# Eight gathers on SyncE instead of four, with table parts loaded in between

## The chip, the core and the metric

The kernel runs on one core of a Trainium2 chip. The metric is the device time of one execution in microseconds (us), as a median over runs. The core has five engines that run their own instruction streams in order: TensorE (PE; its weight loads are PEld), VectorE (DVE), ScalarE (ACT), GpSimd (POOL) and SyncE (SP, which here only issues DMA transfers). They meet at semaphores. Sixteen DMA engines move data between the memory of the chip (HBM) and the on-chip buffers.

## What is computed

A sequence of item numbers `seq` (1024 users, 50 steps) picks rows of 128 numbers from a table with 100001 rows, of which row 0 counts as zero:

```python
e = emb[seq]                                   # 1024 x 50 x 128
prefix = jnp.cumsum(e, axis=1)
uF = prefix / jnp.minimum(t_idx, lengths)      # running mean
y = (uF - mean) * rsqrt(var + eps) * gamma + beta   # mean, var over the users
# 50 steps of: v = v + (x - v) / 2; spike = v >= 1; v = v - spike
uF_out = spikes.mean(axis=0)                   # 1024 x 128
scores = uF_out @ emb.T                        # 1024 x 100001, float32
```

The output has 409.6 MB, and all of the table (51 MB) is read once for the last product, besides the single rows that the 51200 item numbers pick.

## The kernel before

The work has two stages.

In the first stage a loop over t = 0 to 49 (L300) makes one step at a time. `gather(t)` (L201) fills the tile e of 128 x 1024 with the rows of the 1024 items of step t. It does so with eight indirect DMAs, one for each block of 128 users, which GpSimd issues (L204). Two such tiles exist (pool gather, two buffers), so GpSimd works on step t + 1 while step t is used. PE transposes each block into the running sums `pre` in PSUM (L313, eight transposes, the first four into one half and the last four into the other). VectorE scales the two halves and takes their statistics (L322, L323), aggregates them (L333), and a chain of small VectorE and ScalarE instructions makes the normalised input and the new state v (L337 to L359). In the last step (t = 49) the spikes of the step before are taken first (L307, L308), and then the two halves. PE also adds a correction for row 0 (`correct`, L268), which needs `zT`, made at the start.

At the start of the stage VectorE compares idx with zero (L220), PE transposes the result (L223), ScalarE copies it (L225), VectorE makes a tile rb of reciprocal lengths (L240), and PE transposes that (L243). The tiles isz and rb of this start come from the same pool as e; the gathers of step 1 go into the buffer that rb used, and wait for L243.

SyncE issues in this order: the item numbers idx (L171), the lengths, row 0, gamma and beta (L173 to L178), then six DMAs of 3 MB each that bring the first 36 parts of the table (a part is 1024 rows, 0.5 MB) into the tiles rows (`fetch`, L97), and after them single rows. For t = 44 to 47 the block of the first 128 users is not gathered by GpSimd: SyncE reads four item numbers of a user into registers (L189), and issues one DMA of one row (512 bytes) for each (L197), into four tiles aside. So 128 register loads of four values and 512 row loads. Each SyncE DMA uses one of eight semaphores in turn, and waits until the DMA that used it before has landed.

In the second stage the table parts are transposed and split in two (`prepare`, L133; parts 0 and 1 already in steps 42 and 44 of the first stage), multiplied with the spike counts (`product`, L146), scaled into tiles o (L471, L473), and stored by SyncE (`store`, L157). The first store comes from L408, at the end of the first stage. Later parts of the table are fetched on ScalarE's queue.

The order of the instructions on each engine is the order in which the program writes them.

Of the kernel before, what the change touches and what calls it, by code (L numbers as in the profile page):

```python
# [12 lines left out]
F32 = mybir.dt.float32  # L13
BF16 = mybir.dt.bfloat16
F32R = mybir.dt.float32r
I32 = mybir.dt.int32
U32 = mybir.dt.uint32
AF = mybir.ActivationFunctionType
ALU = mybir.AluOpType

P = 128
# [5 lines left out]
GROUP = 6  # L27
AHEAD = 6

WIDTHS = [2, 2, 2, 3, 3, 3, 3] + 12 * [6] + [4, 4]  # L30
NARROW, MIDDLE = 3, 7


@with_exitstack
def rec_kernel(
# [9 lines left out]
    nc = tc.nc  # L45
    B, T = seq.shape
    N, D = table.shape
# [25 lines left out]
    rows = {}  # L73
# [6 lines left out]
    def size(q):  # L80
        return min(HALF, N - q * HALF)

    def group(g):
        at = g if g < AHEAD else AHEAD - 2 + g % 2
        r = rowp.tile([P, GROUP, HALF], F32, tag=f"rows{at}", name=f"rows_{g}")
        for k in range(GROUP):
            rows[g * GROUP + k] = r[:, k, :]
        return r

    def fetch(r, q, n):  # L90

        engine = nc.sync if q < AHEAD * GROUP else nc.scalar
        k = q % GROUP
        n = min(n, parts - q)
        whole = n - (size(q + n - 1) < HALF)
        if whole:
            engine.dma_start(  # L97
                out=r[:, k : k + whole, :],
                in_=table[q * HALF : (q + whole) * HALF, :].rearrange("(q p k) d -> p q (k d)", p=P, k=KQ),
            )  # L100
        if whole < n:
            full, rest = divmod(size(parts - 1), P)
            c1 = (parts - 1) * HALF
            r = r[:, k + whole, :].rearrange("p (k d) -> p k d", d=D)
            if full:
                engine.dma_start(
                    out=r[:, :full, :],
                    in_=table[c1 : c1 + full * P, :].rearrange("(k p) d -> p k d", p=P),
                )
            if rest:  # L110
                engine.dma_start(out=r[:rest, full, :], in_=table[c1 + full * P : N, :])
# [49 lines left out]
    with ExitStack() as ph:  # L161
        once = ph.enter_context(tc.tile_pool(name="once", bufs=1))
        lp = ph.enter_context(tc.tile_pool(name="lif", bufs=2))
        sp = ph.enter_context(tc.tile_pool(name="stats", bufs=3))
        up = ph.enter_context(tc.tile_pool(name="uF", bufs=2))
        gp = ph.enter_context(tc.tile_pool(name="gather", bufs=2))
        accp = ph.enter_context(tc.tile_pool(name="acc", bufs=1, space=bass.MemoryType.PSUM))
        vp = ph.enter_context(tc.tile_pool(name="v", bufs=1, space=bass.MemoryType.PSUM))

        idx = once.tile([P, NB, T], I32, tag="idx", name="idx")  # L170
# [5 lines left out]
        gb = once.tile([P, 2], F32, tag="gb", name="gb")  # L176
        nc.sync.dma_start(out=gb[:, 0:1], in_=gamma.rearrange("(d o) -> d o", o=1))
        nc.sync.dma_start(out=gb[:, 1:2], in_=beta.rearrange("(d o) -> d o", o=1))  # L178
        for g in range(AHEAD):
            fetch(group(g), g * GROUP, GROUP)  # L180

        aside = {}
        for t0, many in ((T - 6, 4),):
            for t in range(t0, t0 + many):
                aside[t] = once.tile([P, P], F32, tag=f"aside{t}", name=f"aside_{t}")
            for p in range(P):
                _, items = nc.values_load_multi_w_load_instructions(  # L189
                    idx[p : p + 1, 0, t0 : t0 + many],  # L190
                    engines=[mybir.EngineType.SP],
                    min_val=0,
                    max_val=N - 1,
                    skip_runtime_bounds_check_because="items are rows of the table; the transfer checks its own bounds",
                )
                for j, item in enumerate(items):
                    nc.sync.dma_start(out=aside[t0 + j][p : p + 1, :], in_=table[bass.ds(item, 1), :])  # L197

        es = {}

        def gather(t):  # L201
            es[t] = gp.tile([P, B], F32, tag="e", name=f"e_{t}")
            for n in range(t in aside, NB):
# [3 lines left out]
                    in_=table,  # L207
                    in_offset=bass.IndirectOffsetOnAxis(ap=idx[:, n, t : t + 1].bitcast(U32), axis=0),
                )
# [52 lines left out]
        def only(t):  # L262

            l = sp.tile([P, D], F32R, tag="l", name=f"l_{t}")
            nc.scalar.activation(l, r0n, AF.Copy, scale=sel[:, t : t + 1])
            return l
# [33 lines left out]
        for t in range(T):  # L300
# [35 lines left out]
            r = sp.tile([P, 1], F32, tag="r", name=f"r_{t}")  # L336
            nc.scalar.activation(r, mv[:, 1:2], AF.Sqrt, bias=eps)  # L337
            nc.scalar.activation(uF, uF, AF.Identity, bias=mv[:, 0:1], scale=-1.0)

# [11 lines left out]
            a = sp.tile([P, 1], F32, tag="a", name=f"a_{t}")  # L351
# [3 lines left out]
            def x(vt, cs):  # L355
                nc.scalar.activation(vt, uF[:, cs], AF.Identity, bias=hgb[:, 1:2], scale=a)  # L356

# [41 lines left out]
        for q, (pool, tag, po) in enumerate(((gp, "e", sums), (up, "uF", [po1[:, cs] for cs in halves]))):  # L399
            o = pool.tile([P, HALF], F32, tag=tag, name=f"o_0_{q}")  # L400
# [26 lines left out]
    for c, W in enumerate(WIDTHS):  # L427
# [30 lines left out]
        for n in range(NB):  # L458
            if c == 0 and n == 0:
                continue  # L460
            pool, tag, most = turns[blocks % len(turns)]
            blocks += 1
            o = pool.tile([P, most * HALF], F32, tag=tag, name=f"o_{c}_{n}")
# [21 lines left out]
            if n in (1, 4) and c >= MIDDLE and to_fetch < parts:  # L485
                g = to_fetch // GROUP
# [26 lines left out]
```

## Time and profile before

| what | before |
|---|---|
| median of 3 runs | 1779.58 us (1778.25 to 1783.5) |
| span of the profiled execution | 1569.9 us |
| POOL busy | 374.6 us in 402 instructions |
| DVE busy | 940.7 us in 1161 instructions |
| PE busy | 1153.1 us in 4548 instructions |
| DMA | 488.25 MB, mean 311 GB/s |

The span goes from the first to the last instruction of the profiled execution. The run times are longer than it by what lies around it; the profiled execution has no time of its own beside its span. In the rows of a timeline the first number is the start in us from the span's start, the second the duration, then engine, source line, operation, output and inputs, sizes, and in brackets the idle time of the engine before it and what ended it. An engine name with a q (SPq) is that engine's own instruction queue.

### The profile page before, as it was taken

To read this page: it belongs to the slowest core of one execution; us is meant where nothing else is said; L and a number is where in the kernel's file an instruction comes from. 1 tells how busy PE (TensorE), PEld (TensorE's weight loads), DVE (VectorE), ACT (ScalarE), POOL (GpSimd) and SP (SyncE) were. 2 spreads that over 40 slices of the span, in tenths; PEclk is the share of its full clock that TensorE was granted. 3 is DMA by queue.
4 is the path that set the end of the run, shared out by engine and by line. 5 is a ranking of instruction groups with operands and counts; after the bars stand their busy time and mean duration, and the time that the engine had idled before them with its cause. 6 is when DMAs were issued, how large, how long until landed. Compare 5 with 4: busy or idle time off the path is not lost.

```text
span 1569.9 us, 14231 instructions
## 1 busy us (share of the span) xinstructions
PE 1153.1 (73%) x4548; PEld 822.3 (52%) x4548; DVE 940.7 (60%) x1161; ACT 630.6 (40%) x700; POOL 374.6 (24%) x402
## 2 busy tenths in 40 slices
PE   4555555555556988899878788887788888788784
PEld 2222222222233766677666666666666666666563
DVE  4777777777778665576545555555555545555453
ACT  2322222222233554465444444444444444444342
POOL 6777777777775000000000000000000000000000
PEclk7555555555555999999999988999999998989998
DMA  9622222222222999999999999999999999999998
GB/s 342 245 55 53 55 54 54 54 53 54 52 53 64 399 411 420 420 393 428 425 432 427 429 428 424 418 422 424 428 413 420 415 424 429 421 423 409 394 423 354
DMA packets 54600, 488.25 MB, mean 311 GB/s; under 512 B 12443, under 2 KB 13756, under 8 KB 33276
## 3 DMA queue, kind: packets, MB, share of 16 engines
q1 hardware_dynamic: 33008, 429.03, 65.1%
q0 software_dynamic: 12672, 25.98, 6.2%
q10 hardware_dynamic: 8844, 32.33, 5.2%
q8 instruction: 36, 0.59, 0.1%
q14 instruction: 40, 0.33, 0.1%
HBM read 77.69 MB, written 409.60 MB: 310 GB/s over the span
## 4 chain that ended last, share of the span: by engine, by line
DMA 52%; POOL 17%; PE 11%; issue 9%; ACT 5%; DVE 4%; DVEq 0%; ACTq 0%; SPq 0%; POOLq 0%
DMA scores<-o 49%; POOL e L204 17%; PE po L149 9%; ACT o L473 5%; DMA e<-in_L_rec_emb_table,idx 3%; DVE o L471 2%; PE pt L119 1%; DVE bs L323 1%; DVE uF L322 0%; DVE s L343 0%; PE pre L313 0%; PE sums L281 0%; DMA idx<-in_r_seq 0%; ACT hi L141 0%; ACT pairs L141 0%
## 5 line engine op out<-in xcount | busy, mean ns | idle before, releaser
L471 DVE TENSOR_SCALAR o<-po 128x1024 f32<-128x1024 f32 x391 | 463.5, 1220 | 351.8 <-DMA scores<-o 323.4
L473 ACT ACTIVATE o<-po 128x1024 f32<-128x1024 f32 (+1 forms) x391 | 387.9, 1018 | 547.8 <-DMA scores<-o 344.9
L204 POOL DMA_INDIRECT e<-in_L_rec_emb_table,idx x396 | 373.9, 944 | 123.4 <-issue 114.6
L149 PE MATMUL po<-pairs,countB 128*128 128x512 f32 x1168 | 314.7, 415 | 67.6 <-ACT o L473 50.7
L149 PEld LDWEIGHTS po<-pairs,countB 128*128 128x128 f32 x1168 | 225.8, 198 | 132.5 <-ACT o L473 65.8
L149 PE MATMUL po<-pairs,countC 128*128 128x512 f32 x876 | 239.1, 419 | 43.6 <-ACT o L473 43.6
L313 PE MATMUL pre<-ident,e 128*128 128x128 f32 x396 | 153.1, 450 | 143.8 <-DMA e<-in_L_rec_emb_table,idx 142.2
L149 PEld LDWEIGHTS po<-pairs,countC 128*128 128x128 f32 x876 | 170.1, 200 | 89.7 <-ACT o L473 54.7
L313 PEld LDWEIGHTS pre<-ident,e 128*128 128x128 f32 x396 | 78.5, 201 | 236.1 <-DMA e<-in_L_rec_emb_table,idx 214.7
L142 DVE TENSOR_TENSOR pairs<-pt,pairs 128x1024 fp32r<-128x1024 f32 (+1 forms) x73 | 88.3, 1217 | 96.6 <-ACT pairs L141 96.5
L337 ACT ACTIVATE r<-mv,eps 128x1 f32<-128x1 f32 x50 | 14.7, 295 | 300.6 <-DVE mv L333 300.6
L322 DVE SCALAR_TENSOR_TENSOR uF<-rlen,pre 128x512 f32<-128x512 f32 x100 | 68.3, 683 | 103.8 <-PE pre L313 103.8
L119 PE MATMUL pt<-ident,rows 128*128 128x128 f32 x782 | 113.5, 293 | 8.0 <-ACT o L473 3.9
L119 PEld LDWEIGHTS pt<-ident,rows 128*128 128x128 f32 x782 | 102.6, 154 | 28.8 <-issue 10.0
L149 PE MATMUL po<-hi,countB 128*128 128x512 f32 x200 | 82.8, 414 | 18.8 <-ACT o L473 13.8
L281 PE MATMUL sums<-s,ident_h 128*128 128x512 bf16 x98 | 49.6, 608 | 60.6 <-DVE s L343 60.6
L270 PE MATMUL pre<-zT,l 128*128 128x512 f32 x100 | 78.0, 782 | 21.6 <-DVE uF L322 21.5
L149 PE MATMUL po<-lo,countB 128*128 128x512 f32 x200 | 80.4, 402 | 0.0
L141 ACT CAST pairs<-pt 128x1024 fp32r<-128x1024 f32 (+1 forms) x73 | 73.6, 1008 | 16.2 <-PE pt L119 15.9
L149 PE MATMUL po<-pairs,countA 128*128 128x512 f32 (+1 forms) x292 | 73.2, 393 | 9.1 <-ACT o L473 9.1
L149 PE MATMUL po<-hi,countC 128*128 128x512 f32 x150 | 62.7, 418 | 16.4 <-ACT o L473 16.4
L356 ACT ACTIVATE v<-uF,hgb,a 128x1024 f32<-128x1024 f32 x49 | 59.2, 1208 | 37.4 <-DVE a L352 37.4
(78 smaller groups left out, 821.1 us busy)
## 6 DMA issues: line engine op xcount, KB each, us to landing
scores<-o SPq DMA_DIRECT2D x96, 3072.0 KB
scores<-o SPq DMA_DIRECT2D x32, 1536.0 KB
rows<-in_L_rec_emb_table ACTq DMA_DIRECT2D x20, 1536.0 KB
scores<-o SPq DMA_DIRECT2D x22, 1024.0 KB
rows<-in_L_rec_emb_table SPq DMA_DIRECT2D x6, 3072.0 KB
scores<-o SPq DMA_DIRECT2D x8, 2048.0 KB
scores<-o SPq DMA_DIRECT2D x8, 1872.5 KB
aside<-in_L_rec_emb_table SPq DMA_DIRECT2D x512, 0.5 KB
```

Source lines behind the costliest of these rows:

```text
L119: nc.tensor.transpose(pt[:, k0 : k0 + kw], r[:kw, k0 : k0 + D], ident[:kw, :kw])
L141: nc.scalar.copy(vh, vp)
L142: nc.vector.tensor_tensor(vl, vp, vh.bitcast(F32), ALU.subtract)
L149: nc.tensor.matmul(po[:, :kw], lhsT=counts[n], rhs=part[:, k0 : k0 + kw], start=j == 0, stop=j == 1,)
L204: nc.gpsimd.indirect_dma_start(out=es[t][:, n * P : (n + 1) * P], out_offset=None, in_=table, in_offset=bass.IndirectOffsetOnAxis(ap=idx[: ...
L270: nc.tensor.matmul(pre[h], lhsT=l, rhs=zT[:, h * BANK : (h + 1) * BANK], start=t == 0, stop=False, skip_group_check=True,)
L281: nc.tensor.matmul(sums[h], lhsT=ident_h, rhs=s[:, h * BANK : (h + 1) * BANK], start=t == 0, stop=t == T - 2, skip_group_check=True,)
L313: nc.tensor.matmul(pre[h][:, k : k + P], lhsT=aside[t] if h == k == 0 and t in aside else e[:, h * BANK + k : h * BANK + k + P], rhs=ident ...
L322: nc.vector.scalar_tensor_tensor(uF[:, cs], rlen[:, cs], 1.0 / (t + 1), pre[h], ALU.max, ALU.mult)
L356: nc.scalar.activation(vt, uF[:, cs], AF.Identity, bias=hgb[:, 1:2], scale=a)
L471: nc.vector.tensor_scalar_mul(o[:, h0 : h0 + hw], po[:, :hw], 1.0 / T)
L473: nc.scalar.mul(o[:, h0 : h0 + hw], po[:, :hw], 1.0 / T)
```

## The change

Eight steps (t = 7, 13, 19, 25, 31, 37, 43 and 49) instead of four leave the first block of 128 users to SyncE. Their item numbers come by an additional small DMA into a tile few (8 partitions x 128 numbers), and VectorE multiplies them by 512, the bytes of a row. SyncE loads sixteen of these byte addresses into registers at a time, and uses them directly as starts in a byte view of the table. The aside tiles come from a pool of three buffers. The first 36 table parts are issued one by one (36 DMAs of 0.5 MB instead of six of 3 MB), spread evenly between the row loads. `gather` and the rest of the kernel are unchanged; the condition in `gather` and in the loop of t picks the steps from the dictionary `aside`. `group` and `fetch` are those of before.

```diff
--- before.py
+++ after.py
@@ -15,6 +15,7 @@
 F32R = mybir.dt.float32r
 I32 = mybir.dt.int32
 U32 = mybir.dt.uint32
+U8 = mybir.dt.uint8
 AF = mybir.ActivationFunctionType
 ALU = mybir.AluOpType
 
@@ -29,6 +30,8 @@
 
 WIDTHS = [2, 2, 2, 3, 3, 3, 3] + 12 * [6] + [4, 4]
 NARROW, MIDDLE = 3, 7
+
+ASIDE, EVERY, MANY = 8, 6, 16
 
 
 @with_exitstack
@@ -164,6 +167,7 @@
         sp = ph.enter_context(tc.tile_pool(name="stats", bufs=3))
         up = ph.enter_context(tc.tile_pool(name="uF", bufs=2))
         gp = ph.enter_context(tc.tile_pool(name="gather", bufs=2))
+        asidep = ph.enter_context(tc.tile_pool(name="aside", bufs=3))
         accp = ph.enter_context(tc.tile_pool(name="acc", bufs=1, space=bass.MemoryType.PSUM))
         vp = ph.enter_context(tc.tile_pool(name="v", bufs=1, space=bass.MemoryType.PSUM))
 
@@ -176,25 +180,38 @@
         gb = once.tile([P, 2], F32, tag="gb", name="gb")
         nc.sync.dma_start(out=gb[:, 0:1], in_=gamma.rearrange("(d o) -> d o", o=1))
         nc.sync.dma_start(out=gb[:, 1:2], in_=beta.rearrange("(d o) -> d o", o=1))
-        for g in range(AHEAD):
-            fetch(group(g), g * GROUP, GROUP)
-
-
-
+        held = [group(g) for g in range(AHEAD)]
+        to_hold = 0
+
+
+        steps = list(range(T - 1 - EVERY * (ASIDE - 1), T, EVERY))
+        few = once.tile([ASIDE, P], I32, tag="few", name="few")
+        with nc.allow_non_contiguous_dma(reason="a few columns of item numbers, once"):
+            nc.sync.dma_start(out=few, in_=seq[:P, steps[0] : T : EVERY].rearrange("p t -> t p"))
+        nc.vector.tensor_single_scalar(few, few, 4 * D, ALU.mult)
+        flat = table.rearrange("n d -> (n d)").bitcast(U8)
         aside = {}
-        for t0, many in ((T - 6, 4),):
-            for t in range(t0, t0 + many):
-                aside[t] = once.tile([P, P], F32, tag=f"aside{t}", name=f"aside_{t}")
-            for p in range(P):
-                _, items = nc.values_load_multi_w_load_instructions(
-                    idx[p : p + 1, 0, t0 : t0 + many],
+        for g, t in enumerate(steps):
+            aside[t] = asidep.tile([P, D], F32, tag="aside", name=f"aside_{t}")
+            for p0 in range(0, P, MANY):
+                while to_hold * ASIDE * P <= (g * P + p0) * AHEAD * GROUP and to_hold < AHEAD * GROUP:
+                    fetch(held[to_hold // GROUP], to_hold, 1)
+                    to_hold += 1
+                _, at = nc.values_load_multi_w_load_instructions(
+                    few[g : g + 1, p0 : p0 + MANY],
                     engines=[mybir.EngineType.SP],
                     min_val=0,
-                    max_val=N - 1,
-                    skip_runtime_bounds_check_because="items are rows of the table; the transfer checks its own bounds",
+                    max_val=(N - 1) * 4 * D,
+                    skip_runtime_bounds_check_because="these are starts of rows of the table; the transfer checks its own bounds",
                 )
-                for j, item in enumerate(items):
-                    nc.sync.dma_start(out=aside[t0 + j][p : p + 1, :], in_=table[bass.ds(item, 1), :])
+                for k, byte in enumerate(at):
+                    nc.sync.dma_start(
+                        out=aside[t][p0 + k : p0 + k + 1, :].bitcast(U8),
+                        in_=flat[bass.ds(byte, 4 * D)].rearrange("(o b) -> o b", o=1),
+                    )
+        while to_hold < AHEAD * GROUP:
+            fetch(held[to_hold // GROUP], to_hold, 1)
+            to_hold += 1
 
         es = {}
```

## The prediction

> **What bounds the kernel now.** I read the page first, then the rows of tile e, then the timelines of the two ends of the first stage, then SyncE's rows.
>
> ```profile
> span 1569.9 us, 14231 instructions
> ...
> POOL 6777777777775000000000000000000000000000
> ...
> DMA  9622222222222999999999999999999999999998
> ...
> DMA scores<-o 49%; POOL e L204 17%; PE po L149 9%; ACT o L473 5%; DMA e<-in_L_rec_emb_table,idx 3%; DVE o L471 2%; PE pt L119 1%; DVE bs L323 1%; DVE uF L322 0%; DVE s L343 0%; PE pre L313 0%; PE sums L281 0%; DMA idx<-in_r_seq 0%; ACT hi L141 0%; ACT pairs L141 0%
> ```
>
> There are two stages. Up to slice 13 (about 500 us) POOL works at a steady share and the DMA engines at 20%; after it POOL is idle and the DMA engines stand at 90% or more with the stores of the scores (49% of the chain). The change touches only the first stage. I take the 1063 us from the first store (506.8) to the end as unchanged, since the stores bound them.
>
> ```profile
> L204 POOL DMA_INDIRECT e<-in_L_rec_emb_table,idx x396: 940/944/1162, 4.3 to 497.6; - x198
> ...
>   issue: 114.6, 376
> ...
> DMA to landing us min/median/max: 2.4/2.5/6.8
> ```
>
> 396 gathers from 4.3 to 497.6 us: 0.944 us busy and 0.30 us of "issue" each, no other wait of weight. (497.64 − 4.30) / 395 = 1.249 us per gather: POOL never stops and sets the pace, 8 gathers or 9.98 us a step.
>
> ```profile
> 490.18 0.48 PE L313 MATMUL pre<-ident,e 128*128 128x128 f32 x1 [0.76 <-DMA e<-in_L_rec_emb_table,idx]
> ...
> 497.64 0.94 POOL L204 DMA_INDIRECT e<-in_L_rec_emb_table,idx  x1 [0.30 <-issue]
> ...
> 498.25 1.22 DVE L308 TENSOR_TENSOR negv<-s,v 128x1024 f32<-128x1024 bf16 x1
> ...
> 500.26 0.47 PE L313 MATMUL pre<-ident,e 128*128 128x128 f32 x1 [0.89 <-DMA e<-in_L_rec_emb_table,idx]
> ...
> 500.77 0.69 DVE L322 SCALAR_TENSOR_TENSOR uF<-rlen,pre 128x512 f32<-128x512 f32 x1
> ...
> 506.78 65.38 SPq L158 DMA_DIRECT2D scores<-o  x30
> ```
>
> This is the end of the stage. The last transpose of step 48 starts at 490.18 (call it X). From there VectorE works without a gap through step 48's tail to L308, which ends at 499.47; only then can it take both halves of step 49 (second half at 500.77). The last transpose of step 49 ends at 500.73, so gathers and VectorE arrive together. Up to X the stage is POOL's; from X on it is VectorE's as well.
>
> ```profile
> 1.04 0.91 DVE L218 MEMSET isz<- 128x1024 f32 x1 [1.04 <-PEq L501]
> ...
> 3.83 33.42 SPq L97 DMA_DIRECT2D rows<-in_L_rec_emb_table  x6
> 4.13 0.65 DVE L220 TENSOR_SCALAR isz<-idx 128x400 f32<-128x400 int32 x2 [2.18 <-DMA idx<-in_r_seq]
> 4.30 1.16 POOL L204 DMA_INDIRECT e<-in_L_rec_emb_table,idx  x1 [2.99 <-DMA idx<-in_r_seq]
> ...
> 10.30 1.97 PE L243 MATMUL rps<-ident,rb 128*128 128x128 f32 x8 [3.43 <-DVE rb L240]
> ...
> 13.26 0.94 POOL L204 DMA_INDIRECT e<-in_L_rec_emb_table,idx  x1 [0.30 <-issue]
> ...
> 14.51 0.94 POOL L204 DMA_INDIRECT e<-in_L_rec_emb_table,idx  x1 [0.30 <-issue]
> ```
>
> VectorE waits for idx (issued at 0.76), compares at 4.13, and a chain over PE, ACT and DVE ends in the transposes L243 at 12.27. POOL's ninth gather (14.51) writes the buffer that these transposes read, so it may not start before they end. Today that leaves 2.2 us of slack.
>
> **What the Trainium skill says.** "DMA: Bandwidth & Descriptors", Latency and other measured facts, gives a register load (tensor_load) a floor of about 600 ns, amortised by loading four at a time. "Runtime: NRT & Kernel Launch", Instruction fetch mechanics, says about 200 ns per register even in bulk, for loads from HBM. They pull apart: a floor makes sixteen values nearly as cheap as four, a price per register does not. The trace has four values from SBUF at 564 ns: below the floor, and 141 ns per register, so it decides nothing. The DMA page, Why a DMA increments its semaphore by 16 and not by 1, says that the engine count is the largest up to 16 that divides the slowest dimensions: the new few load (8 x 128) would run on 8 engines; no load of before has this shape.
>
> **The change, part by part.**
> *Gathers removed.* Before, steps 44 to 47 skip one gather each; after, steps 7, 13, ..., 43, 49. Up to X it is 4 before and 7 after: 3 x 1.249 = 3.7 us earlier. The eighth (step 49) lies after X: its 1.25 us on POOL are hidden behind VectorE, which is late next. Value 0, at most 1.25.
>
> *The start.* The few load (1024 pieces of 4 bytes) goes out at 3.83, in the place of the first table load, and VectorE's first instruction is now its multiplication. Behind it in VectorE's queue stand L218 and L220, for which PE, ACT and, by the buffer, POOL wait. idx (1024 pieces) took 3.37 us from issue to its user, len_i (1024 pieces of 4 bytes, by semaphore events) 3.07; few so lands at 6.9 to 7.2, and up to 8.6 if half the engines double the 1.5 us of its pieces. I take 7.4. Then multiplication about 0.2 (an estimate from the row of L233, 0.23), memset 0.91, and the compare starts at 8.6 instead of 4.13: 4.5 late. L243 ends at 16.8, the ninth gather starts at 16.9 instead of 14.51. Cost 2.4 us, bounds 1.9 to 3.6; below nothing is excluded, because POOL has no idle time later to win it back.
>
> ```profile
> L189 SPq TENSOR_LOAD <-idx x128: 457/564/737, 37.3 to 354.3; - x128
> L197 SPq FUSED_REGOPS  x512: 37/37/51, 37.9 to 356.2; - x171
> L197 SPq MOVE aside<-in_L_rec_emb_table x512: 29/29/29, 38.0 to 356.2; - x171
> L197 SPq DMA_DIRECT2D aside<-in_L_rec_emb_table x512: 224/225/7507, 38.0 to 356.3; - x171
> 100.15 256.36 SPq L197 DMA_DIRECT2D aside<-in_L_rec_emb_table  x441
> ```
>
> *SyncE.* 441 row loads took 256.36 us: 0.581 each. By start times in the trace a load is FUSED_REGOPS to MOVE 73 ns, MOVE to DMA 60, DMA to the next 276; a TENSOR_LOAD takes 564 + 54, and 46 more in what follows. 4 x 409 + 664 = 2.30 us for four; a pause of some 0.35 us about every 23 us makes the rest. After: the scaling on chip removes the FUSED_REGOPS, so sixteen loads cost 16 x 336 = 5.38, plus 0.10, plus T, the TENSOR_LOAD of sixteen. 64 of these: 350 + 64 T. The table parts: 36 DMAs of 128 runs, like the gb loads at 0.43 + 0.05: 17. Each SyncE DMA waits for the eighth before it; a row lands 1.1 to 1.5 us after issue and eight take 2.7, a 0.5 MB part needs about 3.2 (1.5 at the 342 GB/s of slice 1, plus start and receipt) against 3.2 and a TENSOR_LOAD: no wait. Pauses: 7. Sum S = 374 + 64 T, starting at 7.7.
>
> *When it must be ready.* The last group (step 49) has to land so that four transposes (1.4 us) end when VectorE is free, 499.5 − 1.3: at 496.8. With 1.4 to land, S may be 487.7, so T may be 1.78 us. The earlier groups need their rows every 58.6 us (47 gathers), looser than that because the first has until about 80 us. If T is 0.56, S is 410; if T grows by register (16 x 0.141 = 2.26), S is 519 and the stage ends 31 us late; at the page's 0.2 per register T is 3.2 and it would be 91. I take T = 1.2, between the trace's fixed and proportional readings: S = 451, last row at 460, hidden behind POOL with 37 us to spare. If that cover goes, each 0.1 us of T costs 6.4.
>
> *Table parts in between, three aside buffers, multiplication.* The parts 0 and 1 are wanted at step 42 and 44 (over 400 us), the rest in the second stage; the last is issued at about 450: nothing. A buffer is reused 18 steps later, after PE read it 100 us before: nothing. Gathers meet a 1.5 us part now and then, and have a whole step of buffer: nothing. The multiplication itself is counted above.
>
> **Sum.** −3.7 + 2.4 = −1.3 us: span 1568.6 against 1569.9. The median of the runs, 1779.58, lies 209.7 above the profiled span; I take that as constant: 1778.3.
>
> **The rivals.**
> A, forecast: SyncE keeps up, the start costs 2.4: 1778.3; own range 1774 to 1782. 0.52.
> B, slower: the TENSOR_LOAD of sixteen is priced by the register. Place: SyncE, between groups; it decides from T = 1.78, and at 2.26 gives −1.3 + 31 = +30: 1809 (at T = 2.0, 1794). For it: the price per register, and 564 / 4. Against: 564 is below a floor of 600 for one. 0.35.
> C, the start does not cost (few lands early or the ninth gather is not held), and perhaps the tail gives its 1.25: −3.7 to −5.0: 1775.2. For it: only that 2.2 us of slack exist; against: the queue order on VectorE. 0.10.
> D, the change does not do what it says: the byte-typed copies go out as 512 pieces instead of one 512-byte run. At the 9 ns of a 4-byte piece that is 4.6 us for each of 1024 loads, 4.2 ms more. Against: a contiguous row was one piece before. 0.03.
>
> **How the numbers follow.** What a measurement can tell from no change is about 0.3%, 5.3 us. A and C lie inside it (their gains are 1.3 to 5.0), 0.62, of which I give 0.05 to faster, since C stands at the edge and the runs shown spread over 5 us; B beyond T = 1.86 and D make slower 0.36; a B between 1.78 and 1.86 stays in same. Same 0.59. The range runs from 1774 (C) to 1808, which takes in most of B; A's own is given above.
>
> **What would show it.** Right: SyncE's rows at about 0.42 us a load and ending near 460; the TENSOR_LOAD at 0.6 to 1.7; compare L220's start near 8.6 and the ninth gather near 16.9; POOL ending 4 gathers less 2.4, so 2.6 us, before its old 498.6; the first store near 505.5. Wrong: PE or POOL waiting for a DMA of tile aside, a SyncE row that runs past 496, a TENSOR_LOAD over 1.8, more packets under 512 B than the few load adds, or a second stage of another length than 1063 us.

## The result, and the profile after

The changed kernel took 1847.1 us (median, 1843.5 to 1849.5) against 1779.3 for the kernel before: a ratio of 1.0365, interval 1.0341 to 1.0388, 68 us slower. The forecast was 1778.3 and no change. Without a difference in the program, the kernel before takes 1780 us in all runs of some sessions and 1571 in all runs of others: this comparison is of the first kind, and the profile of before that the prediction was read from is of the second.

The page of the changed kernel, in the session of the comparison (span, then busy tenths of POOL in 40 slices of 46 us):

```profile
span 1846.3 us, 14730 instructions
...
POOL 6646363626262626100000000000000000000000
```

The profiled execution took 1848.0 us, and its span is 1846.3. So 1.7 us lie outside the span, not 209.7 (1.7 to 1.9 in every run that has both on record). POOL, before a steady 7 to slice 12, now swings between 6 and 2 to 4 and lasts to slice 17. The second stage has its old length: from the first store, at 782.98, to the end are 1063.3 us (1063.1 in the profile of before). The loss is in the first stage.

The list of who waited for whom (us in total, times, longest):

```profile
PE pre L330 <- DMA aside<-in_L_rec_emb_table: 244.9, 8, 36.4
...
POOL e L221 <- PE pre L330: 197.7, 7, 31.2
```

PE waits for each of the eight aside tiles, up to 36 us, and GpSimd then stands behind PE, because its two buffers are full. SyncE's timeline (start, duration, count) shows why the tiles are late:

```profile
28.73 51.37 SPq L208 DMA_DIRECT2D aside<-in_L_rec_emb_table  x32
...
111.55 11.63 SPq L208 DMA_DIRECT2D aside<-in_L_rec_emb_table  x32
...
782.98 14.88 SPq L161 DMA_DIRECT2D scores<-o  x11
```

Both upper rows are 32 loads of one row each. The first runs beside GpSimd's gathers: 51.37 us, 1.6 us a row. The second lies in a stretch in which GpSimd stands still, and with it PE and VectorE: 11.63 us, 0.36 a row. The instructions are of the same kind, and so are the transfers. The rows by instruction (minimum, median, maximum in ns):

```profile
L200 SPq TENSOR_LOAD <-few x64: 3/1166/1245, 7.9 to 767.3; - x64
```

```profile
L208 SPq MOVE aside<-in_L_rec_emb_table x1024: 1/29/1412, 9.1 to 773.4; - x171
L208 SPq DMA_DIRECT2D aside<-in_L_rec_emb_table x1024: 2/228/1424, 9.2 to 773.5; - x171
```

The medians are as small as one could wish: a register load of sixteen takes 1.17 us and a DMA issue 0.23. It is the maxima that tell: even a MOVE between registers, which waits for no semaphore, takes up to 1412 ns. Beside gathers 603 of 1080 SyncE instructions start within 0.3 us after the one before, 235 start 0.6 to 0.8 us after it, and 176 start 1.2 to 1.5 us after it. MOVEs and DMA issues of rows are hit alike: after 204 of 517 and 192 of 516 of them the next instruction takes more than 0.55 us to come (0 and 6 of 1024 in after_again, a later run of the same kernel without the delays).

### The profile page after: what moved, and what is told of

Same layout as the page of the kernel before. It is cut to its first block, busy times and chain, and to the rows that moved or that the text cites. A ratio compares the mean times of both kernels' runs of the same rounds, so it can differ in the third digit from the quotient of the medians.

```text
span 1846.3 us, 14730 instructions
## 1 busy us (share of the span) xinstructions
PE 1106.3 (60%) x4538; PEld 830.4 (45%) x4548; DVE 940.5 (51%) x1162; ACT 630.5 (34%) x700; POOL 370.8 (20%) x398
## 4 chain that ended last, share of the span: by engine, by line
DMA 42%; PE 8%; ACT 4%; SPq 2%; DVE 2%; issue 2%; DVEq 0%; ACTq 0%
DMA scores<-o 42%; PE po L152 8%; ACT o L490 4%; SPq L208 2%; DVE o L488 2%; SPq L200 0%; ACT pairs L144 0%; PE pt L122 0%; DVE pairs L145 0%; ACTq L490 0%; DVE bs L340 0%; DMA aside<-in_L_rec_emb_table 0%; DVE uF L339 0%; PE sums L152 0%; DVEq L526 0%
## 5 line engine op out<-in xcount | busy, mean ns | idle before, releaser
L221 POOL DMA_INDIRECT e<-in_L_rec_emb_table,idx x392 | 370.1, 944 | 376.8 <-PE pre L330 197.7
L152 PE MATMUL po<-pairs,countC 128*128 128x512 f32 x876 | 241.9, 423 | 48.4 <-ACT o L490 48.2
L339 DVE SCALAR_TENSOR_TENSOR uF<-rlen,pre 128x512 f32<-128x512 f32 x100 | 67.9, 679 | 368.1 <-PE pre L330 234.2
L287 PE MATMUL pre<-zT,l 128*128 128x512 f32 x100 | 72.6, 728 | 228.0 <-DVE uF L339 197.1
L330 PE MATMUL pre<-ident,aside 128*128 128x128 f32 x8 | 3.6, 450 | 244.9 <-DMA aside<-in_L_rec_emb_table 244.9
L287 PEld LDWEIGHTS pre<-zT,l 128*128 128x128 f32 x100 | 27.1, 272 | 268.4 <-issue 165.2
L330 PE MATMUL pre<-ident,e 128*128 128x128 f32 x392 | 95.7, 419 | 9.4 <-issue 6.2
L330 PEld LDWEIGHTS pre<-ident,e 128*128 128x128 f32 x392 | 84.2, 226 | 29.2 <-issue 24.5
L298 PE MATMUL sums<-s,ident_h 128*128 128x512 bf16 x88 | 45.4, 607 | 62.7 <-issue 36.8
```

The source lines that it names most:

```text
L152: nc.tensor.matmul(po[:, :kw], lhsT=counts[n], rhs=part[:, k0 : k0 + kw], start=j == 0, stop=j == 1,)
L221: nc.gpsimd.indirect_dma_start(out=es[t][:, n * P : (n + 1) * P], out_offset=None, in_=table, in_offset=bass.IndirectOffsetOnAxis(ap=idx[: ...
L287: nc.tensor.matmul(pre[h], lhsT=l, rhs=zT[:, h * BANK : (h + 1) * BANK], start=t == 0, stop=False, skip_group_check=True,)
L298: nc.tensor.matmul(sums[h], lhsT=ident_h, rhs=s[:, h * BANK : (h + 1) * BANK], start=t == 0, stop=t == T - 2, skip_group_check=True,)
L330: nc.tensor.matmul(pre[h][:, k : k + P], lhsT=aside[t] if h == k == 0 and t in aside else e[:, h * BANK + k : h * BANK + k + P], rhs=ident ...
L339: nc.vector.scalar_tensor_tensor(uF[:, cs], rlen[:, cs], 1.0 / (t + 1), pre[h], ALU.max, ALU.mult)
```

## The experiments

**The kernel before, again.** No edit.

> The kernel before, unchanged, to see where its 1779 us go, since its profile on record spans only 1569.9 us. Theory S (SyncE's row loads and GpSimd's gathers hinder each other whenever they run together, in the kernel before too; its profile on record was an execution in which that did not happen): span about 1777 us, the aside rows last until far beyond 500 us, GpSimd waits for PE behind a late aside tile. Theory O (the 209.7 us lie outside the span, as I took it): span 1570 us.

It took 1786.1 us in its one run, and the before beside it 1780.8 (median of 7 runs). Its page, its wait for aside, and SyncE's timeline and rows:

```profile
span 1784.2 us, 14221 instructions
...
POOL 6666666666650015000000000000000000000000
```

```profile
PE pre L313 <- DMA aside<-in_L_rec_emb_table: 135.5, 1, 135.5
```

```profile
37.90 623.39 SPq L197 DMA_DIRECT2D aside<-in_L_rec_emb_table  x512
719.04 1.23 SPq L158 DMA_DIRECT2D scores<-o  x2
```

```profile
L197 SPq FUSED_REGOPS  x512: 2/37/1413, 37.3 to 660.9; - x171
L197 SPq MOVE aside<-in_L_rec_emb_table x512: 2/29/1408, 37.4 to 661.0; - x171
L197 SPq DMA_DIRECT2D aside<-in_L_rec_emb_table x512: 2/225/7567, 37.9 to 661.1; - x171
```

Theory O is out, and what S gave for this run is there. POOL falls to 0 in the middle of the stage: after step 43 everything waits 135.5 us for SyncE, whose 512 rows last 623 us (318 in the profile that the prediction was read from). Here too a MOVE takes up to 1408 ns. In sessions of this kind the kernel before pays for its row loads too; the profile on record shows an execution in which it does not.

**No row loads at all.** The same session.

```diff
-        for t0, many in ((T - 6, 4),):
+        for t0, many in ():
```

> The kernel before without any SyncE row loads: all 400 gathers on GpSimd. Theory S: nothing hinders GpSimd, 400 x 1.249 = 500 us of gathers, the first store at about 512 us, 1575 us in all, 200 us less than before. Theory O: five microseconds more than before, 1785 us.

1651.9 us, ratio to before 0.9271 (0.9247 to 0.9295): 129 us faster with four gathers more. So the row loads were a loss there. But it isn't the 1575 of theory S: something holds the stage up without any row load. The rows of tile e on POOL (below the first line: idle time before it, by what ended it):

```profile
L204 POOL DMA_INDIRECT e<-in_L_rec_emb_table,idx x400: 938/944/1164, 4.2 to 566.3; - x134
...
  issue: 112.5, 369
  remote: 65.9, 16
```

GpSimd waits 66 us in pieces of 3 to 4.5 us, each before the first gather of a step (from 84 us on mostly of every third step), the one that may not start before PE has left its buffer; the release itself is missing in the record ("remote"). On average that makes (566.3 − 4.2) / 399 = 1.41 us a gather, not 1.249, though the gathers themselves still take 0.944 us and most follow each other at 1.25. What is late is PE and VectorE:

```profile
40.37 1.91 PE L313 MATMUL pre<-ident,e 128*128 128x128 f32 x8
...
46.66 0.69 DVE L322 SCALAR_TENSOR_TENSOR uF<-rlen,pre 128x512 f32<-128x512 f32 x1 [3.63 <-remote]
```

All eight transposes of the step end at 42.28 by the profile, and VectorE, idle for 3.63 us, takes their result only at 46.66. In the profile of before the same hand-over took some 0.03 us (a transpose that ended at 490.66, L322 at 490.69). So SyncE's loads are not the origin of the delays; they suffer from them too.

**The old form of a load, and the table parts first.** The first takes back the byte addresses and the loads of sixteen together, the second the place of the table parts; the same session, one run each.

```diff
-ASIDE, EVERY, MANY = 8, 6, 16
+ASIDE, EVERY, MANY = 8, 6, 4
...
-        nc.vector.tensor_single_scalar(few, few, 4 * D, ALU.mult)
...
-                        out=aside[t][p0 + k : p0 + k + 1, :].bitcast(U8),
-                        in_=flat[bass.ds(byte, 4 * D)].rearrange("(o b) -> o b", o=1),
+                        out=aside[t][p0 + k : p0 + k + 1, :],
+                        in_=table[bass.ds(byte, 1), :],
```

> The changed kernel with the old form of a row load: four item numbers at a time, multiplied on SyncE, float32 rows; steps, table parts and buffers as in the change. Theory S: the form matters little, since the delay comes with any SyncE work beside gathers: 1850 to 1910 us. Rival (the byte addresses or the loads of sixteen make SyncE stall): SyncE at 0.58 us a row again, all rows in by 620 us, 1690 us.

```diff
-        held = [group(g) for g in range(AHEAD)]
-        to_hold = 0
+        for g in range(AHEAD):
+            fetch(group(g), g * GROUP, GROUP)
...
-                while to_hold * ASIDE * P <= (g * P + p0) * AHEAD * GROUP and to_hold < AHEAD * GROUP:
...
-        while to_hold < AHEAD * GROUP:
...
```

> The changed kernel with the six 3 MB table loads first, as before, instead of 36 between the row loads. Theory S: no gain, 1840 to 1860 us. Rival (the table parts between the row loads are what stalls SyncE): rows at 0.42 us after the first 65 us, 1575 to 1585 us.

2023.7 and 1884.0 us. Neither rival holds: with the old form the time is 177 us longer than the 1847.1 of the change, and without parts in between it is 37 us longer, not shorter. Both lie above what theory S gave (1850 to 1910, and 1840 to 1860), for two different reasons. In the second run the small load of few stands behind the six 3 MB loads in SyncE's order:

```profile
56.18 0.21 DVE L191 TENSOR_SCALAR few<-few 8x128 int32<-8x128 int32 x1 [56.18 <-DMA few<-in_r_seq]
...
65.74 0.94 POOL L215 DMA_INDIRECT e<-in_L_rec_emb_table,idx  x1 [51.70 <-PE rps L254]
```

VectorE gets few at 56.18, the rows start at 57.7 instead of 9.2, and GpSimd waits 51.7 us before the ninth gather. This late start is enough for the 37 us, so they are no price of the place of the parts; the pace of the rows is that of the change (1.04 and 1.03 us below).

In the first run the form of a load matters. What the old form has more of is instructions: 3.25 for a row (TENSOR_LOAD / 4, FUSED_REGOPS, MOVE, DMA) against 2.06. These are SyncE's instructions over the stretches with gathers (gaps of more than 8 us between gathers left out; the last column counts the issues of table parts too):

| kernel | instructions a row | us a row beside gathers | us an instruction |
|---|---|---|---|
| b_again | 3.25 | 1.72 | 0.53 |
| after_old_form | 3.25 | 1.48 | 0.45 |
| after | 2.06 | 1.03 | 0.49 |
| after_parts_first | 2.06 | 1.04 | 0.50 |

The time goes roughly with the instructions. That is theory I of the next expectations; its rivals are that the 512-byte transfers are what is held up (D), or that the loss is in proportion to the rows (L).

**One instruction a row, and half of the rows.** fixed_rows has 1024 transfers of the same size, but from rows that are fixed in the program, so no register load, no MOVE, no few and no multiplication; four_steps has ASIDE, EVERY = 4, 12.

```diff
-        few = once.tile([ASIDE, P], I32, tag="few", name="few")
...
-                _, at = nc.values_load_multi_w_load_instructions(
...
-                        in_=flat[bass.ds(byte, 4 * D)].rearrange("(o b) -> o b", o=1),
...
+                    row = 97 * (g * P + p0 + k)
+                    nc.sync.dma_start(out=aside[t][p0 + k : p0 + k + 1, :], in_=table[row : row + 1, :])
```

> The changed kernel with the same 1024 row loads, but of rows that are fixed when the program is written: one SyncE instruction per row instead of two and a share of a register load. The rows are not those that the item numbers ask for. Theory I (cost per SyncE instruction): about 0.5 us a row beside gathers, all rows in by 550 us or so, hardly a wait, 1640 to 1680 us. Rival D (the 512-byte transfers themselves are what is held up beside the gathers): a row still takes 1.0 us, 1830 to 1850 us.

> The changed kernel with four steps (13, 25, 37, 49) instead of eight, everything else as in the change: 512 row loads in the new form. Theory I (beside gathers every SyncE instruction takes about 0.5 us, of whatever kind, so a row in the new form takes about 1.0 us instead of the 0.42 of my sum; GpSimd itself needs 1.42 us a gather): 512 rows take about 530 us plus 36 parts, just inside the 560 us of the gathers, no or hardly any wait for aside rows, 1640 to 1665 us. Rival L (delay grows with the number of rows at SyncE in the same way everywhere, half the rows half the loss): 1750 us.

1568.7 and 1575.8 us, beside a before of 1571.7. All bounds were missed, those of I and of its rivals: the delay wasn't there at all. It is these two runs that showed that before has two times.

> 1024 rows of fixed numbers, one SyncE instruction each (the rows are not those that the item numbers ask for). Where before takes 1571.7: 3.0 us less, as it was. Where before takes 1780: theory I (0.5 us per SyncE instruction beside gathers) all rows in by 550 us, 1640 to 1680 us; rival D (the transfers are what is held up) 1830 to 1850 us.

> The change with four steps in place of eight. Where before takes 1571.7: 4 us more than before, as it was (1 gather more before the last state, 2.7 for the start). Where before takes 1780: theory I, rows at 1.0 us are in by 560 us, hardly a wait, 1640 to 1665 us; rival L (loss in proportion to the rows) 1750 us.

1568.6 us (ratio 0.9981, 0.9975 to 0.9988) and 1574.6 (1.0025, 1.0016 to 1.0035), beside a before of 1571.3: as expected for such a session, and they say nothing on I.

> 1024 rows of fixed numbers, one SyncE instruction each (the rows are not those that the item numbers ask for). Where before takes 1780: theory I (0.5 us per SyncE instruction beside gathers) all rows in by 550 us, 1640 to 1680 us; rival D (the 512-byte transfers are what is held up) 1830 to 1850 us. Where before takes 1571.7: 1568.6 again, which tells nothing new.

> The change with four steps in place of eight. Where before takes 1780: theory I, rows at 1.0 us are in by 560 us, hardly a wait, 1640 to 1665 us; rival L (loss in proportion to the rows) 1750 us. Where before takes 1571.7: 1574.5 to 1575.8 again.

1569.2 and 1577.0, beside 1571.2: inconclusive again.

> 1024 rows of fixed numbers, one SyncE instruction each (the rows are not those that the item numbers ask for). Where before takes 1780: theory I (0.5 us per SyncE instruction beside gathers) all rows in by 550 us, 1640 to 1680 us; rival D (the 512-byte transfers are what is held up) 1830 to 1850 us. Where before takes 1571: 1568.6 again.

> The change with four steps in place of eight. Where before takes 1780: theory I, rows at 1.0 us are in by 560 us, hardly a wait, 1640 to 1665 us; rival L (loss in proportion to the rows) 1750 us. Where before takes 1571: 1574.5 to 1577 again.

Beside a before of 1780.3 (one run of each): 1672.6 and 1659.2 us, both inside the times of theory I; D (1830 to 1850) and L (1750) are out. SyncE's row in fixed_rows_4, and PE's whole wait for aside in four_steps_4:

```profile
L198 SPq DMA_DIRECT2D aside<-in_L_rec_emb_table x1024: 1/250/1458, 4.1 to 598.2; - x171
```

```profile
PE pre L330 <- DMA aside<-in_L_rec_emb_table: 8.7, 1, 8.7
```

With one instruction a row, a row takes 0.60 us beside gathers; with 2.06 it takes 1.11. The same two programs needed 0.35 and 0.44 us a row where before takes 1571. So the delay adds 0.25 us to a row of one instruction and 0.66 us to a row of two. Theory I is not exact: fixed_rows_4 has its last row at 598.2 instead of 550, and PE still waits for aside six times, 58.5 us in all, instead of hardly at all. With half the rows the wait shrinks from 244.9 us to 8.7, not to a half: 512 rows fit beside the gathers, and 1024 don't.

**A third buffer for gathered rows** (bufs=3, no row loads) was to show how much of the 66 us is GpSimd's waiting for a buffer.

> All 400 gathers on GpSimd, as in no_aside (1652 us), with three instead of two tiles for the gathered rows. If GpSimd only loses time because a late PE or VectorE holds its buffer now and then, a third one takes most of the 66 us of such waits away: 1585 to 1610 us. Rival (the steps themselves take as long on VectorE and PE on average): 1645 to 1655 us.

It ran beside a before of 1571.7 us and took 1576.5: 4.8 more, for four gathers more at 1.25. In that session there was no such wait to remove, so the question stays open.

**The change where before takes 1571 us, and with few moved back.**

> The changed kernel, unchanged. The kernel before has been seen at 1780 us beside it and at 1571.7 us in another session on the chip, without one instruction being different. Where before takes 1571.7: my sum of the prediction holds for it (3 gathers less, the start 2.4 to 2.7 later), so 1.0 to 1.3 us less than before, rows of 0.42 us at SyncE. Where before takes 1780: 1847 again, for the rows then take 1.0 us beside gathers (theory I). Rival R (the change costs 68 us in either session): 1640 us where before takes 1571.7.

> The changed kernel with the multiplication of few moved behind the reciprocal lengths in VectorE's order, so that the compare of idx does not wait for the few load; SyncE starts its rows some 7 us later. Where before takes 1571.7: the start's 2.7 us come back, 3.0 to 4.0 us less than before, 1568 us. Rival: the ninth gather is late for another reason, 1570.5 as the change. Where before takes 1780: no difference from 1847 that matters, since 68 us are lost at SyncE.

after_again took 1571.65 us against 1571.31: ratio 0.9999 (0.9991 to 1.0008), so the gain of 1.0 to 1.3 us can't be told from none, and rival R is out. It is the same program as the 1847 us. Its page, its start, SyncE's rows, and the end of its first stage:

```profile
span 1570.6 us, 14740 instructions
...
POOL 6777777777774000000000000000000000000000
```

```profile
7.42 0.32 DVE L191 TENSOR_SCALAR few<-few 8x128 int32<-8x128 int32 x1 [7.42 <-DMA few<-in_r_seq]
...
8.74 0.66 DVE L237 TENSOR_SCALAR isz<-idx 128x400 f32<-128x400 int32 x2
...
14.77 1.97 PE L260 MATMUL rps<-ident,rb 128*128 128x128 f32 x8 [3.27 <-DVE rb L257]
...
17.01 0.94 POOL L221 DMA_INDIRECT e<-in_L_rec_emb_table,idx  x1 [3.05 <-PE rps L260]
```

```profile
L208 SPq MOVE aside<-in_L_rec_emb_table x1024: 29/29/38, 9.0 to 444.4; - x171
L208 SPq DMA_DIRECT2D aside<-in_L_rec_emb_table x1024: 227/228/357, 9.1 to 444.4; - x171
```

```profile
495.23 0.94 POOL L221 DMA_INDIRECT e<-in_L_rec_emb_table,idx  x1 [0.30 <-issue]
...
497.11 1.22 DVE L325 TENSOR_TENSOR negv<-s,v 128x1024 f32<-128x1024 bf16 x1
...
497.75 0.48 PE L330 MATMUL pre<-ident,e 128*128 128x128 f32 x1 [0.83 <-DMA e<-in_L_rec_emb_table,idx]
...
499.57 0.67 DVE L339 SCALAR_TENSOR_TENSOR uF<-rlen,pre 128x512 f32<-128x512 f32 x1
...
505.84 1.23 SPq L161 DMA_DIRECT2D scores<-o  x2
```

Here the MOVE never takes more than 38 ns, a register load of sixteen takes 1.17 us as in the other session, and the last row goes out at 444.4. The compare of idx starts at 8.74, the ninth gather at 17.01. At the end the last transpose is done at 498.2, and VectorE, busy to 498.33 with L325, takes the second half only at 499.57.

few_later moves the multiplication (and with it SyncE's loads) behind rb:

```diff
-        nc.vector.tensor_single_scalar(few, few, 4 * D, ALU.mult)
...
         nc.vector.tensor_copy(rb, rl.unsqueeze(2).to_broadcast([P, NB, P]))
+        nc.vector.tensor_single_scalar(few, few, 4 * D, ALU.mult)
```

```profile
4.06 0.65 DVE L214 TENSOR_SCALAR isz<-idx 128x400 f32<-128x400 int32 x2 [2.11 <-DMA idx<-in_r_seq]
...
10.09 0.34 DVE L235 TENSOR_SCALAR few<-few 8x128 int32<-8x128 int32 x1
...
14.44 0.94 POOL L198 DMA_INDIRECT e<-in_L_rec_emb_table,idx  x1 [0.30 <-PE pre L331]
```

The compare is back at 4.06, few is scaled at 10.09, and the ninth gather goes out at 14.44. 1567.84 us, ratio 0.9979 (0.9971 to 0.9986): 3.5 less than before, inside the 3 to 4 expected, and a little faster than both kernels in that session. It wasn't run where before takes 1780; there no_aside and four_steps are the ones that beat both.

## Why the prediction was wrong

The step that failed is the one under "Sum": "The median of the runs, 1779.58, lies 209.7 above the profiled span; I take that as constant". It is not outside the span. In b_again 1784.2 of 1786.1 us are span, and nearly all of the difference is in the first stage: the first store at 719.0 instead of 506.8. I had read a profile of one execution and forecast others that are 210 us longer, and had put their difference where nothing could touch it. From that follow the sizes that were off, as measured in the comparison and in sessions of its kind:

- "POOL never stops and sets the pace", 1.249 us a gather: 1.40 to 1.45 there on average, waits left out that are longer than 8 us, and it stops.
- A row of 0.42 us at SyncE: 1.03 beside gathers. S was to be 451 us, ending at 460; the last row goes out at 773.5, and PE waits for aside, which the prediction had named as a sign that it is wrong.
- Rival B had the right place (SyncE late, PE waiting for aside) and the wrong price: it put the break at a register load of 1.78 us. That load took 1.17, as I had taken it (1.2). What broke the cover was the delay of MOVEs and DMA issues.
- The 68 us: in b_again the last of 512 rows goes out at 661.1, and six steps follow to the first store at 719.0 (57.9 us). With 1024 rows it is 773.5, and one step follows to 783.0 (9.5 us). So 112.4 us for the rows, less 48.4 for the steps that no longer follow them: 64.0 us between the first stores (62.1 between the two spans; the medians are 68 apart, and the execution of b_again is 5 us over the 1780.8 beside it). Rows spread over the stage cost less after the last one, but there are twice as many.

Where the profile was of the same kind as the runs, the parts of the sum came out (after_again): multiplication of few at 7.4 predicted, 7.42 measured; ninth gather at 16.9 and 17.01; rows 0.42 and 0.43; last row at 460 and 444.4; GpSimd's end 2.6 earlier and 2.4; first store 505.5 and 505.84. The total of −1.3 lies inside the interval (−1.4 to +1.3 us), which holds no change as well. That the eighth gather is hidden behind VectorE is seen in L325 and L339 above. That the start costs some 2.5 is shown by few_later: the ninth gather goes out 2.57 us earlier than in after_again, for a move of the multiplication and what follows from it (the runs differ by 3.8, part of it in the second stage). four_steps fits too: it has as many gathers as before but one step aside after X, so a gather more ahead of it (1.25) beside the start (2.4 to 2.7), a loss of 3.7 to 4.0; it lost 4.1 and 3.2, and 5.8 in a single run.

Two slips of the working changed nothing: at T = 2.0 rival B comes to 1793 us by its own sum, not 1794, and it leaves the band of 5.3 us at T = 1.88, not 1.86.

The prediction took T = 1.2 between a floor (the Trainium skill, "DMA: Bandwidth & Descriptors", Latency and other measured facts: about 600 ns, which the compiler amortises by unrolling four times) and a price per register ("Runtime: NRT & Kernel Launch", Instruction fetch mechanics: about 200 ns, from HBM). The traces have 564 ns for four values and 1166 for sixteen; a line through these two is some 50 ns a value over 360 (an estimate): closer to the first, below its figure at four values.

What stays open is where the delays come from. They occur while gathers run: in the 135.6 us of b_again without a gather SyncE needs 0.58 us a row, as in the profile of before. But PE and VectorE stand still in that stretch too, so it is not shown that the gathers are what matters. SyncE's loads are not needed (no_aside), and the program does not decide, since the same one has both times. Before stood at 1780 in three sessions and at 1571 in three, and one chip showed both within twenty minutes. The granted TensorE clock does not tell them apart (0.52 up to 490 us in the profile of before, 0.54 up to 700 us in b_again).

One thing in the traces goes with the time: the seven with the delays hold 728 to 1069 semaphore events of the engines between 100 and 340 us, and the ten others 3758 to 5520. So a rival stands untested: that the recording of the execution is itself what holds the instructions up. No run is known to have been made without recording, so the record can't settle it.

## What to carry to other kernels

Before using a profile, compare its span with the times of the runs. Here 1.7 to 1.9 us lay outside the span of a run; a difference of 209.7 us meant that the profile was of another kind of execution, and a sum made from it could not forecast the runs.

Work that is moved to a second engine, to run beside the first, has to be priced beside that engine and not from the medians of its instructions. Where before takes 1780 us, the time roughly followed the number of SyncE's instructions for the rows (after_parts_first with its late start aside): 0 in no_aside (1652 us), 1024 in fixed_rows (1673) and 1056 in four_steps (1659), 1664 in before (1780), 2112 in the change (1847), 3328 in the old form (2024). Where before takes 1571 us, this order is gone: four_steps (1575) is slower there than the change (1572). One profile can't tell which of the two a program will meet.

A small load whose consumer stands first in an engine's queue delays everything behind it: here 2.5 us, won back by moving one line, and 51.7 us where the load itself stood behind large ones.

## What the runs showed of the hardware that was not expected

Beside indirect gathers, in some sessions, SyncE's instructions took 0.45 to 0.58 us on average, register MOVEs as much as DMA issues, against 0.2 to 0.34 us in the others (0.43 us for a row with 2.06 instructions, 0.35 for a row with one); over half of them were not delayed at all, and the median of a register load was the same (1.17 us for sixteen values in both). PE and VectorE stood idle for up to 9.4 us at a time in no_aside. There, with no row loads at all, GpSimd came to 1.41 us a gather instead of 1.249 by waiting for them, with its gathers unchanged at 0.944 us. A register load of sixteen values took twice as long as one of four (1.17 and 0.56 us), not four times.
